# Row statistics in attention: two ScalarE passes in place of VectorE's bn_stats

## The chip, the cores and the metric

The kernel runs on one core of one Trainium2 chip. A time is the device time of one execution in microseconds (us). TensorE multiplies matrices (its rows in the profile are PE, its weight loads PEld), VectorE (DVE) and ScalarE (ACT) work element by element, GpSimd (POOL) does small operations and issues the indirect transfers, and SyncE (SP) issues the other DMAs. Each engine executes its own instructions in order and waits for others by semaphores.

## The reference

One block of a transformer over x of 8 batches x 1024 rows x 256 columns, all in float32:

```
x = x + 0.5 * ffn(layernorm(x))
x = x + attention(layernorm(x))
x = x + 0.5 * ffn(layernorm(x))
layernorm(x): (x - mean) / sqrt(var + 1e-5), over the 256 columns, no weights
ffn: a router (256 x 8, softmax, argmax) picks one of 8 experts for a row;
     an expert takes its first 320 rows, in the order of rows; the others go through a shared layer
     both are relu(x @ w1 + b1) @ w2 + b2, hidden width 1024
attention: 16 heads of width 16; xd = x @ W_down; keys, queries, values from xd per head;
     softmax(q k^T) v over the 1024 rows of a batch; out @ W_unify + b_unify
```

Each of the three layers needs the mean and the variance of every row of x as it stands then: 64 tiles of 128 rows for each layer, eight tiles in a batch.

## The kernel before, in words

**Stages.** The first feed-forward (about 0 to 660 us of the profile), the attention stage (the first exp at 659.9 us, the last at 2452.3), the second feed-forward (to 2945.7). The last blocks of the first feed-forward carry the first steps of attention beside them (`first_pair`).

**Attention** (`run`). A pair n (0 to 31) is one group of four heads of one batch: batch b = n // 4, group g = n % 4. A pair has 16 units u: for half q = u // 8 of the queries and block c = u % 8 of the keys, TensorE computes the scores of four heads (`psc`, L985, three matmuls a head, four heads on four quarters of the array's rows), ScalarE takes the exp (`ex`, L994, four a unit), and TensorE weighs the values one unit later (`av`, L1016). In the same units it computes the scores of the *next* pair in the other order (`pm`), of which VectorE takes the row maxima (`halves`, L1001, four a unit); these are subtracted in the next pair. `psc` and the projections of the next batch share four banks of PSUM, `pm` and the router's and unify's sums three others. At the end of a half VectorE turns the result (`turned`, L1031), POOL divides it (`ot`, L1039), and VectorE turns it back (`ho`, L1051).

**Work beside it.** Other work is cut into steps by Python generators, which stand in the list `beside` with a pair by which they must be done and the kind of their next step: ARRAY (TensorE), DVE or POOL. A step yields the kind of the step after it. `run` takes one step of a kind at given units: an ARRAY step where the unit is in `slots[0]` and such a step is due (this sets `other`), a DVE step where it is in `slots[1]`, a POOL step in units without an ARRAY step. The kinds with the earliest due pair go first, and `done_by(n)` takes all that is still due at a pair's end, without regard to units. The engines' order inside attention is this order of the program, written out by hand for PE, ACT and DVE; POOL and SP are ordered by the scheduler.

The generators: `prepare(b + 1)` (normed rows on POOL, transposes `ptan`, projections `pxd`, `pq`, `pv`, each evicted by ScalarE; the k and q rows go to DRAM by SP and are fetched two pairs ahead), queued when g is 0; `unify(b - 1)` (`pu`, added to x by VectorE at L1069), also when g is 0; `route(b - 1)`, the router of the second feed-forward, queued when g is 1 with four pairs' time; and `stats(b)` for batches 4 to 7, queued at the start. Batch 7 has no batch to prepare after it.

**The row statistics** (`norm_steps`, L141 on). For each of a batch's eight tiles VectorE does a bn_stats and a bn_aggr (L148, L149), one tile a DVE step; then it computes 1 / sqrt(var + eps) by a shift and four Newton steps (L156 to L173) on 128x8 numbers. `stats` calls it for attention, `route` for the router in attention, and `Layer.route` for the router outside it (the first feed-forward's, and batch 7 of the second).

**The router's steps** after the statistics: four normed tiles on POOL (`rn`), transposes (`ptrn`) and copies, the other four, logits (`pl`, L1089), then `places`: a chain of small operations between VectorE, POOL and TensorE that finds each row's slot (`places`, `behind`, `slot`, L289 to L346), and eight normed tiles with an indirect DMA each on POOL (`send`, L361), which put the rows into their slots in DRAM. For batch 6 this runs in pairs 29 to 31, and its sends follow pair 31. In the second feed-forward the tiles of the hidden layer (`h_o`, L470, L474) lie in memory that attention's pools have used.

Of the kernel before, what the change touches and what calls it, by code (L numbers as in the profile page):

```python
# [10 lines left out]
F32 = mybir.dt.float32  # L11
# [3 lines left out]
ALU = mybir.AluOpType  # L15
# [25 lines left out]
def macaron(  # L41
# [95 lines left out]

    small = ctx.enter_context(tc.tile_pool(name="small", bufs=3))

    ARRAY, DVE, POOL = 0, 1, 2  # L140

    def norm_steps(name, b, mean, rstd):


        st = small.tile([P, TB, 6], F32, tag="st", name=f"st_{name}")
        mv = small.tile([P, TB, 2], F32, tag="mv", name=f"mv_{name}")
        for t in range(TB):
            nc.vector.bn_stats(st[:, t, :], xs[b][:, t, :])  # L148
            nc.vector.bn_aggr(mv[:, t, :], st[:, t, :])  # L149
            yield DVE  # L150
        nc.vector.tensor_copy(mean, mv[:, :, 0])
        v = small.tile([P, TB], F32, tag="v", name=f"v_{name}")
        nc.vector.tensor_scalar(v, mv[:, :, 1], EPS, None, ALU.add)

        half = small.tile([P, TB], I32, tag="half", name=f"half_{name}")
        nc.vector.tensor_single_scalar(  # L156
            half, v.bitcast(I32), 1, ALU.logical_shift_right
        )
        yi = small.tile([P, TB], I32, tag="yi", name=f"yi_{name}")
        nc.vector.tensor_scalar(  # L160
            yi, half, -1.0, float(0x5F3759DF), ALU.mult, ALU.add
        )
        y = yi.bitcast(F32)
        for i in range(4):
            if i % 2 == 0:
                yield DVE
            a = small.tile([P, TB], F32, tag="a", name=f"a_{name}_{i}")
            nc.vector.tensor_tensor(a, y, y, ALU.mult)
            nc.vector.scalar_tensor_tensor(a, a, -0.5, v, ALU.mult, ALU.mult)
            to = rstd if i == 3 else small.tile(  # L170
                [P, TB], F32, tag="yn", name=f"yn_{name}_{i}"
            )
            nc.vector.scalar_tensor_tensor(to, a, 1.5, y, ALU.add, ALU.mult)  # L173
            y = to
        yield POOL

    def norm_stats(name, b, mean, rstd):
        for _ in norm_steps(name, b, mean, rstd):
            pass

    def normed(pool, tag, name, t, mean, rstd, on=None, numbered=False):
        xn = pool.tile([P, W if numbered else D], F32, tag=tag, name=name)
# [576 lines left out]
    def attention(use, weights, router):  # L759
# [318 lines left out]
        def route(b):  # L1078

            sl = slice(b * TB, (b + 1) * TB)  # L1080
            mean, rstd = router.mean[:, sl], router.rstd[:, sl]
            yield from norm_steps(f"f1_{b}", b, mean, rstd)
            logits = use.pool.tile([P, TB, E], F32, tag="logits", name=f"logits1_{b}")

            def found(q, xnt):
                pl = bank_v(f"pl_{b}_{q}")
                for i in range(4):
                    for k in range(KC):
                        nc.tensor.matmul(  # L1089
                            pl[:, i * E : (i + 1) * E],  # L1090
                            lhsT=xnt[:, k, i * P : (i + 1) * P],
                            rhs=rw_sb[:, k, :],
                            start=(k == 0),
                            stop=(k == KC - 1),
                        )
                    if i == 1:
                        yield
                nc.vector.tensor_tensor(
                    logits[:, 4 * q : 4 * q + 4, :],
                    pl[:, : 4 * E].rearrange("p (t e) -> p t e", e=E),  # L1100
                    rb_sb.unsqueeze(1).to_broadcast([P, 4, E]),
                    ALU.add,
                )
                yield ARRAY if q == 0 else DVE

            yield from rows_transposed("rn", b, mean, rstd, found)
            yield from router.places(b, logits, use.pool, bank_v, nc.gpsimd)
            for t in range(b * TB, (b + 1) * TB):
                xn = normed(
                    use.pool, "send", f"send1_{t}", t, *router.of(t), nc.gpsimd, numbered=True  # L1110
                )
                router.send(t, xn)
                yield POOL

        def stats(b):

            sl = slice(b * TB, (b + 1) * TB)
            yield from norm_steps(f"a{b}", b, amean[:, sl], arstd[:, sl])


        later = []
# [21 lines left out]

        def done_by(n):
            while any(by <= n for by, _, _ in beside):
                for kind in (POOL, DVE, ARRAY):
                    if any(by <= n and what == kind for by, what, _ in beside):
                        step(kind)

        def queue(n):  # L1150

            b, g = divmod(n, G)
            if n + 2 < PAIRS:
                fetch(n + 2)
            if g == 0:
                if b > 0:
                    beside.append([n, ARRAY, unify(b - 1)])
                if b + 1 < B:
                    beside.append([n + 1, POOL, prepare(b + 1)])
            if g == 1 and b > 0:  # L1160
                beside.append([n + 4, DVE, route(b - 1)])

        def ones(i):
            vp = use.pool.tile([P, TB * HEADS * V + S], F32, tag=f"vp{i}", name=f"vp{i}")
# [53 lines left out]
        def run(own):  # L1218
# [3 lines left out]
            ones(1)  # L1222
            for b in range(AHEAD - 1, B):
                reload(b)
                beside.append([G * (b - 1) - 1, DVE, stats(b)])
            last = None

            def weighed(parts=(0, 1)):
# [3 lines left out]
            for n in range(PAIRS):  # L1232
# [8 lines left out]
                for u in range(UNITS):  # L1241
                    todo = {}
                    old = len(later)
                    slots = SLOTS_OF[n % G < 2]
                    if ahead:
                        passes(n, n + 1, u, ORDERS[0], todo)

                        other = u % TB in slots[0] and due(ARRAY) is not None

                        whole = other or u % TB < 2  # L1250
                        weighed((0, 1) if whole else (0,))
                        passes(n, n + 1, u, ORDERS[1], todo)
                        if other:
                            step(ARRAY)
                        elif not whole:
                            weighed((1,))
                    else:

                        passes(n, None, u, ORDER_OF_LAST, todo)
                        weighed()  # L1260
                        other = False
                        if u > 1:
                            step(ARRAY)
                        if u == TB + 3:
                            beside.append([n + 1, ARRAY, islice(unify(B - 1), 2)])
                    if u % TB in slots[1]:
                        step(DVE)
                    if not other:
                        step(POOL)
                    last = (n, u, [todo["ex", h] for h in range(4)])  # L1270
                    afterwards(len(later) - old)
                    if ahead and u % TB == TB - 1:
                        lowest(n + 1, u // TB)
# [131 lines left out]
```

## Time and profile before

| | |
|---|---|
| median of 3 runs | 2952.49 us (2950.14 to 2956.28) |
| profiled execution | 2947.41 us, span 2945.7 us |
| granted TensorE clock | 0.978 (mean) |
| busy: PE, PEld | 2805.4 us (95%), 1549.6 us (53%) |
| busy: DVE, ACT, POOL | 1879.2 us (64%), 1375.5 us (47%), 863.4 us (29%) |

A line of a group reads: line of the kernel, engine, operation, tile written <- tiles read, shape, count | busy time of the group in us, mean ns of one | idle time of the engine just before them, and what ended it. A line of the waits reads: who waited <- for whom: us in total, times, longest. A line of the timeline reads: start in us, duration in us, engine, line, operation, tiles, count, and in brackets the idle time before it with what ended it.

### The profile page before, as it was taken

The numbers are of one execution on the slowest core, as the hardware profiler recorded it, in microseconds if no ns is written. First come the engines' busy times: TensorE is split into PE (matmuls) and PEld (weight loads), VectorE is DVE, ScalarE is ACT, GpSimd is POOL, SyncE is SP. The second block draws the span as 40 slices with busy tenths as digits, with TensorE's granted clock in tenths as the row PEclk, the third lists the DMA queues.
The fourth block names the chain that finished last, engine by engine and source line by source line (L and its number), as shares of the span: only waits on it lengthen the run. The fifth ranks groups of instructions, "written<-read, shape, count | busy, mean of one in ns | idle before, by whom it ended". The sixth has DMA issues, their size and how long they took to land.

```text
span 2945.7 us, 56665 instructions
## 1 busy us (share of the span) xinstructions
PE 2805.4 (95%) x22066; PEld 1549.6 (53%) x22066; DVE 1879.2 (64%) x4177; ACT 1375.5 (47%) x2512; POOL 863.4 (29%) x1144
## 2 busy tenths in 40 slices
PE   4799999899999999999999999999999998999998
PEld 4567776454444444444444444444444445666775
DVE  7344223567998888888888787788787963222221
ACT  1111111207666666766766766766765672111111
POOL 3444433314001034133123221321410215432331
PEclk7799999999999999999999999999999999999999
DMA  8522553415112101301301301301411102311440
GB/s 227 149 85 76 184 186 99 152 38 177 35 49 77 67 27 64 117 24 58 126 24 56 127 24 50 133 24 44 161 38 38 39 3 71 129 60 51 148 148 28
DMA packets 163736, 251.46 MB, mean 85 GB/s; under 512 B 36737, under 2 KB 109698, under 8 KB 163458
## 3 DMA queue, kind: packets, MB, share of 16 engines
q1 hardware_dynamic: 144178, 196.93, 20.6%
q0 software_dynamic: 18432, 50.62, 5.1%
q8 instruction: 177, 2.90, 0.4%
q14 instruction: 101, 0.83, 0.1%
q10 hardware_dynamic: 848, 0.18, 0.0%
HBM read 144.10 MB, written 103.57 MB: 84 GB/s over the span
## 4 chain that ended last, share of the span: by engine, by line
PE 63%; DVE 13%; issue 1%; POOL 1%; DMA 0%; ACT 0%; POOLq 0%; ACTq 0%
PE psc L985 19%; PE av L1016 15%; DVE halves L1001 9%; PE pm L985 7%; PE pe_o L499 5%; PE ph_o L456 5%; PE pe_e L499 2%; PE ph_e L456 2%; PE pu L1061 2%; PE pxd L860 2%; PE pv L892 1%; DVE turned L1031 1%; PE pq L878 1%; PE pl L1089 1%; PE ptrn L830 0%
## 5 line engine op out<-in xcount | busy, mean ns | idle before, releaser
L1001 DVE TENSOR_REDUCE halves<-pm 128x1 f32<-128x512 f32 x2048 | 1309.7, 681 | 258.1 <-PE pm L985 229.0
L994 ACT ACTIVATE ex<-psc 128x512 f32<-128x512 f32 x2048 | 1111.6, 596 | 579.1 <-PE psc L985 574.4
L985 PE MATMUL pm<-k,q 32*128 32x512 f32 x4096 | 872.5, 449 | 47.3 <-DVE halves L1001 38.0
L985 PE MATMUL psc<-q,k 32*128 32x512 f32 x4096 | 794.1, 456 | 2.9 <-PEq L668 2.9
L1016 PE MATMUL av<-ex,vp 128*32 128x256 f32 (+1 forms) x6472 | 614.2, 450 | 0.0
L985 PEld LDWEIGHTS psc<-q,k 32*128 32x128 f32 x4096 | 327.8, 183 | 480.5 <-issue 421.5
L985 PEld LDWEIGHTS pm<-k,q 32*128 32x128 f32 x4096 | 375.5, 184 | 129.8 <-DVE halves L1001 107.1
L985 PE MATMUL psc<-m,ones_r 32*128 32x512 f32 x2048 | 407.9, 390 | 0.0
L456 PE MATMUL ph_o<-bT_o,oa 128*128 128x512 f32 x704 | 321.9, 607 | 9.6 <-DVE h_o L474 8.5
L499 PE MATMUL pe_o<-ob,h_o 128*128 128x256 f32 x1408 | 318.6, 382 | 0.0
L1039 POOL TENSOR_TENSOR ot<-turned,rec 128x256 f32<-128x256 f32 x64 | 39.6, 619 | 886.6 <-DVE rec L1034 880.1
L499 PEld LDWEIGHTS pe_o<-ob,h_o 128*128 128x128 f32 x1408 | 265.5, 191 | 47.2 <-issue 13.5
L1016 PEld LDWEIGHTS av<-ex,vp 128*32 128x32 f32 x6472 | 129.0, 108 | 299.3 <-issue 276.3
L456 PEld LDWEIGHTS ph_o<-bT_o,oa 128*128 128x128 f32 x704 | 133.1, 194 | 164.1 <-issue 149.8
L470 ACT ACTIVATE h_o<-ph_o,ob 128x512 f32<-128x512 f32 x88 | 60.4, 687 | 338.7 <-PE ph_o L456 319.5
L474 DVE TENSOR_SCALAR h_o<-ph_o,ob 128x512 f32<-128x512 f32 x88 | 66.0, 750 | 230.4 <-ACT h_o L470 226.0
L985 PEld LDWEIGHTS psc<-m,ones_r 32*128 32x128 f32 x2048 | 197.7, 185 | 13.3
L509 DVE SCALAR_TENSOR_TENSOR y_o<-pe_o,old_o 128x256 f32<-128x256 f32 x88 | 37.2, 423 | 195.2 <-PE pe_o L499 195.1
L499 PE MATMUL pe_e<-wb,h_e 128*128 128x256 f32 (+1 forms) x640 | 143.9, 381 | 0.0
L456 PE MATMUL ph_e<-bT_e,wa 128*128 128x320 f32 x512 | 140.6, 433 | 1.8 <-ACT bT_e L204 1.8
L204 ACT COPY bT_o<-pt_bT_o 128x1024 f32<-128x1024 f32 x22 | 22.3, 1012 | 241.2 <-PE pt_bT_o L200 241.2
L499 PEld LDWEIGHTS pe_e<-wb,h_e 128*128 128x128 f32 (+1 forms) x640 | 112.9, 179 | 16.4 <-issue 3.1
(181 smaller groups left out, 2395.8 us busy)
## 6 DMA issues: line engine op xcount, KB each, us to landing
k<-krows SPq DMA_DIRECT2D x64, 512.0 KB
wa<-in_w_dram SPq DMA_DIRECT2D x16, 1024.0 KB
wb<-in_w_dram SPq DMA_DIRECT2D x16, 1024.0 KB
krows<-kh SPq DMA_DIRECT2D x32, 512.0 KB
krows<-kl SPq DMA_DIRECT2D x32, 512.0 KB
q<-qrows SPq DMA_DIRECT2D x32, 512.0 KB
rows_o<-buf SPq DMA_DIRECT2D x88, 130.0 KB
x<-in_x_dram SPq DMA_DIRECT2D x8, 1024.0 KB
```

The source lines that it names most:

```text
L456: nc.tensor.matmul(ps[:, i * 512 : i * 512 + width], lhsT=wa[:, k, (m + i) * P : (m + i + 1) * P], rhs=xnt[:, k, c0:c1], start=(k == 0), s ...
L470: nc.scalar.activation(t[:, 0, : hi - lo], ps[:, lo - c0 : hi - c0], AF.Relu, bias=bias[:, m : m + 1],)
L474: nc.vector.tensor_scalar(t[:, 1, : hi - lo], ps[:, 512 + lo - c0 : 512 + hi - c0], bias[:, m + 1 : m + 2], 0.0, ALU.add, ALU.max,)
L499: nc.tensor.matmul(ps[lo - i * P : hi - i * P, :D], lhsT=of[:, lo - a : hi - a], rhs=w[:, m, :], start=(m == 0), stop=(m == MC - 1),)
L509: nc.vector.scalar_tensor_tensor(y[:n, :], ps[:n, :D], 0.5, olds[i][:n, :], ALU.mult, ALU.add)
L860: nc.tensor.matmul(ps, lhsT=wd_sb[:, k, m * P : (m + 1) * P], rhs=xnt[:, k, :], start=(k == 0), stop=(k == KC - 1),)
L985: nc.tensor.matmul(ps, lhsT=lhs, rhs=rhs, start=(len(left) + 1 == todo[kind, h, "of"]), stop=not left,)
L994: nc.scalar.activation(ex, ps, AF.Exp, scale=S ** -0.5)
L1001: nc.vector.tensor_reduce(halves[m][:, t, half, h : h + 1], ps, AX.X, ALU.max, negate=True)
L1016: nc.tensor.matmul(avs[n, q][32 * h : 32 * h + 32, cols], lhsT=vps[b % 2][:, at : at + 2 * S], rhs=ex[:, cols], start=(c == 0), stop=(c == ...
L1039: nc.gpsimd.tensor_tensor(outs_t[q][:, :, at : at + S].rearrange("p (t a) s -> p a t s", t=4), by[:, :, :S].rearrange("p (a t) s -> p a t ...
L1061: nc.tensor.matmul(ps[:, i * D : (i + 1) * D], lhsT=outs[b, g, q][:, at : at + P], rhs=wu_sb[:, g, :], start=(g == 0), stop=(g == G // 2 - 1),
```

## The change

`norm_steps` gets an argument `junk`, a pool. Without one it is as before. With one, the sums of the rows are taken by ScalarE: eight activations with Identity over 128x256, whose accumulator gives the row sums; VectorE makes the mean and its negative of them; eight activations with Square and the negative mean as a bias per partition, whose accumulator gives the sum of squared differences. The activations' outputs go to a tile that nothing reads (tag `zero`, one buffer). They are taken two in a step of a new kind, ACT. The Newton steps on VectorE stay. `stats` of batches 4 to 7 and `route` of batches 0 to 6 pass a pool; the statistics of batches 0 to 3 for attention and those outside attention don't. `run` takes an ACT step in each unit with `other` set, behind its ARRAY and DVE steps, and in each unit of the last pair; `done_by` takes them before the ARRAY steps. `route` is now queued with an ACT step first.

```diff
-    ARRAY, DVE, POOL = 0, 1, 2
+    ARRAY, DVE, POOL, ACT = 0, 1, 2, 3
...
-    def norm_steps(name, b, mean, rstd):
-        st = small.tile([P, TB, 6], F32, tag="st", name=f"st_{name}")
-        mv = small.tile([P, TB, 2], F32, tag="mv", name=f"mv_{name}")
-        for t in range(TB):
-            nc.vector.bn_stats(st[:, t, :], xs[b][:, t, :])
-            nc.vector.bn_aggr(mv[:, t, :], st[:, t, :])
-            yield DVE
-        nc.vector.tensor_copy(mean, mv[:, :, 0])
-        v = small.tile([P, TB], F32, tag="v", name=f"v_{name}")
-        nc.vector.tensor_scalar(v, mv[:, :, 1], EPS, None, ALU.add)
+    def norm_steps(name, b, mean, rstd, junk=None):
+        if junk is None:
...
+        else:
+            total = small.tile([P, 2, TB], F32, tag="total", name=f"total_{name}")
+            lower = small.tile([P, TB], F32, tag="lower", name=f"lower_{name}")
+            for i in range(2):
+                for t in range(TB):
+                    nc.scalar.activation(
+                        junk.tile([P, W], F32, tag="zero", name=f"junk_{name}_{i}_{t}")[:, :D],
+                        xs[b][:, t, :], AF.Square if i else AF.Identity,
+                        bias=lower[:, t : t + 1] if i else 0.0, accum_out=total[:, i, t : t + 1],
+                    )
+                    if t % 2:
+                        yield ACT if t < TB - 1 else DVE
+                if i == 0:
+                    nc.vector.tensor_scalar(lower, total[:, 0, :], -1.0 / D, None, ALU.mult)
+                    nc.vector.tensor_scalar(mean, total[:, 0, :], 1.0 / D, None, ALU.mult)
+                    yield ACT
+            v = small.tile([P, TB], F32, tag="v", name=f"v_{name}")
+            nc.vector.tensor_scalar(v, total[:, 1, :], 1.0 / D, EPS, ALU.mult, ALU.add)
...
-            yield from norm_steps(f"f1_{b}", b, mean, rstd)
+            yield from norm_steps(f"f1_{b}", b, mean, rstd, use.pool)
...
-                for kind in (POOL, DVE, ARRAY):
+                for kind in (POOL, DVE, ACT, ARRAY):
...
-                beside.append([n + 4, DVE, route(b - 1)])
+                beside.append([n + 4, ACT, route(b - 1)])
...
-                beside.append([G * (b - 1) - 1, DVE, stats(b)])
+                beside.append([G * (b - 1) - 1, ACT, stats(b, own)])
...
                     if u % TB in slots[1]:
                         step(DVE)
+                    if other or not ahead:
+                        step(ACT)
                     if not other:
                         step(POOL)
```

More of the change, by code (lines that the diff above doesn't have):

```diff
@@ new lines, in norm_steps @@
+    def norm_steps(name, b, mean, rstd, junk=None):
+        if junk is None:
+            st = small.tile([P, TB, 6], F32, tag="st", name=f"st_{name}")
+            mv = small.tile([P, TB, 2], F32, tag="mv", name=f"mv_{name}")
+            for t in range(TB):
+                nc.vector.bn_stats(st[:, t, :], xs[b][:, t, :])
+                nc.vector.bn_aggr(mv[:, t, :], st[:, t, :])
+                yield DVE
+            nc.vector.tensor_copy(mean, mv[:, :, 0])
+            v = small.tile([P, TB], F32, tag="v", name=f"v_{name}")
+            nc.vector.tensor_scalar(v, mv[:, :, 1], EPS, None, ALU.add)
+        else:
+            total = small.tile([P, 2, TB], F32, tag="total", name=f"total_{name}")
+            lower = small.tile([P, TB], F32, tag="lower", name=f"lower_{name}")
+            for i in range(2):
+                for t in range(TB):
+                    nc.scalar.activation(
[9 more added lines that the diff above has]
+                    yield ACT
+            v = small.tile([P, TB], F32, tag="v", name=f"v_{name}")
+            nc.vector.tensor_scalar(v, total[:, 1, :], 1.0 / D, EPS, ALU.mult, ALU.add)
@@ L175, in norm_steps @@
         yield POOL
-    def norm_stats(name, b, mean, rstd):
-        for _ in norm_steps(name, b, mean, rstd):
-            pass
     def normed(pool, tag, name, t, mean, rstd, on=None, numbered=False):
@@ L1113, in route, with stats @@
                 yield POOL
-        def stats(b):
+        def stats(b, junk=None):
             sl = slice(b * TB, (b + 1) * TB)
-            yield from norm_steps(f"a{b}", b, amean[:, sl], arstd[:, sl])
+            yield from norm_steps(f"a{b}", b, amean[:, sl], arstd[:, sl], junk)
         later = []
```

## The prediction

> **What bounds the kernel now.** I read the page first (busy shares, then the chain that ended last), then the waits and the stretches of single head pairs in the attention stage, then rows by form, then the timeline at the places where the change acts.
>
> ```profile
> PE 2805.4 (95%) x22066; PEld 1549.6 (53%) x22066; DVE 1879.2 (64%) x4177; ACT 1375.5 (47%) x2512; POOL 863.4 (29%) x1144
> PE 63%; DVE 13%; issue 1%; POOL 1%; DMA 0%; ACT 0%; POOLq 0%; ACTq 0%
> L1001 DVE TENSOR_REDUCE halves<-pm 128x1 f32<-128x512 f32 x2048 | 1309.7, 681 | 258.1 <-PE pm L985 229.0
> L994 ACT ACTIVATE ex<-psc 128x512 f32<-128x512 f32 x2048 | 1111.6, 596 | 579.1 <-PE psc L985 574.4
> ```
>
> TensorE is busy 95% of the span and carries most of the chain; VectorE has 13% of it, nearly all through the row maxima (L1001); ScalarE has none, and its exps (L994) nearly always wait for TensorE. The whole change lies in attention (first exp at 659.9 us, last at 2452.3) and its end. Of the waits in attention, these are TensorE's for VectorE:
>
> ```profile
> PEld pm L985 <- DVE halves L1001: 91.5, 143, 1.5
> PE pm L985 <- DVE halves L1001: 37.4, 74, 1.1
> ```
>
> Stretches of three pairs (from the first exp of a pair to that of the next; columns: length, busy PE, PEld, DVE, ACT, POOL):
>
> ```profile
> 775.80:825.80 50.00, 47.77 (x548) 20.76 (x544) 47.14 (x97) 34.76 (x65) 1.24 (x2) 1.00 0.10 35
> 1164.30:1225.60 61.30, 61.14 (x576) 28.15 (x572) 47.39 (x93) 44.73 (x85) 20.34 (x23) 1.00 0.38 131
> 2403.20:2455.00 51.80, 51.80 (x386) 24.23 (x386) 8.75 (x28) 34.01 (x66) 4.16 (x13) 1.00 0.04 12
> ```
>
> Pair 2 has seven row-statistics steps on VectorE and no array work: DVE 47.1 of 50.0, near its limit. Pair 9 has six such steps but eight units with array work: TensorE is busy 61.1 of 61.3, VectorE has 14 us to spare. So the same statistics cost something in one kind of pair and nothing in the other. Pair 31 has no row maxima, and VectorE is idle.
>
> **1. What VectorE loses.** 88 steps of bn_stats and bn_aggr leave it, in eleven batches of statistics (batches 4 to 7 for attention, 0 to 6 for the router):
>
> ```profile
> L148 DVE BATCH_NORM_STATS2 st_f<-x 128x6 f32<-128x256 f32 x58 | 24.2, 417 | 0.0
> L149 DVE BATCH_NORM_AGGREGATE mv_f<-st_f 128x2 f32<-128x6 f32 x58 | 10.6, 182 | 2.0
> L204 ACT COPY bT_e<-pt_bT_e 128x256 f32<-128x256 f32 x8 | 3.0, 378 | 0.0
> L470 ACT ACTIVATE h_e<-ph_e,b 128x256 f32<-128x256 f32 x32 | 15.2, 474 | 51.7 <-PE ph_e L456 51.7
> L470 ACT ACTIVATE kept_e<-ph_e,b 128x64 f32<-128x64 f32 x32 | 10.1, 314 | 17.7 <-DVE h_e L474 17.7
> ```
>
> 88 x (0.417 + 0.182) = 52.7 us; eleven times three small operations come for two (0.17 each), so about 51 us net. What of it is on the path: a plain unit takes 2.93 us from exp to exp and holds 4 x 0.64 = 2.56 us of maxima, so VectorE has 0.37 of slack a unit. A pair without any other work would take about 48.8 us (16 x 2.93, plus 0.7 twice and 0.26 twice at the transposes of a finished half). Against that: pair 2 50.0, pair 3 51.1, pair 29 50.2: 4.9 us to gain together. Pairs 6, 10, ..., 30 (two steps and the Newton steps, 51.9 of which 1.0 is array work): about 1.0 each, 7 us. The pairs with unify, projections or router places after them: about 0.7 a batch from units at the end of a half (3.02 where a step came before, 2.93 where none did) and from work that now falls into array units: 5 us. Gain **17 us**, bounds 0 and 51.
>
> **2. What ScalarE gains.** 176 activations over 128x256, two in a slot, 88 slots; the program order puts a slot behind the unit's four exps and its array copies, and before the next unit's exps. No row has an activation with an accumulator. Main part: 0.38 (the copy of 128x256) in the first pass, 0.47 (h_e, also with a bias per partition) in the second. The read of the accumulator: the Trainium skill says of VectorE (page "VectorE: DVE Perf Modes", section "Two Vector instructions with no wait between them") that an operation that writes its accumulator out is two instructions; if ScalarE is the same, the second costs at least the fixed part of an activation: 596 - 512 x 0.833 = 0.17 (0.833 a column from 314 and 687 at 64 and 512 columns). As one instruction a slot takes 0.76 or 0.95 us, as two 1.1 or 1.3. All write one junk tile, so each waits for the one before; I take **1.1 and 1.3**, with 1.6 and 1.8 as the dear end (the read as dear as the 128x64 row and no overlap).
>
> A second rule speaks against the change. "ScalarE: Activation LUTs", section "What ACT_TABLE_LOAD costs", gives 2.66 us for each switch to another function set. Two switches a slot would make 88 x 2 x 2.66 = 468 us. The profile has one table load in all (1283 ns) under Exp, Relu and copies, and the changed program's ScalarE order holds one load too; I take 0.
>
> How much of a slot is covered is read at the unit after it. Example, behind a unit with the q projection (pair 9, unit 1):
>
> ```profile
> 1173.80 0.62 ACT L847 COPY whole<-pq 128x512 f32<-128x512 f32 x1
> 1174.28 1.13 ACT L994 ACTIVATE ex<-psc 128x512 f32<-128x512 f32 x2
> 1175.60 1.09 ACT L994 ACTIVATE ex<-psc 128x512 f32<-128x512 f32 x2 [0.19 <-PE psc L985]
> 1176.90 1.06 PE L1016 MATMUL av<-ex,vp 128*32 128x512 f32 x8
> ```
>
> The exps follow the copies with no gap, have 0.19 before the second two, and end at 1176.69, 0.21 before TensorE's weighing needs them. Cover 0.41. The medians of the same three gaps by unit, where a plain unit follows: xd projection 0.57, transposes 0.75, values 0.97, no array work 1.08, logits 1.39, unify over 2.3. Where another array unit follows, its weighing comes some 1.5 us later and all is covered. In the order of the changed kernel, slots (first, second pass) followed by a plain unit: xd 9, 11; q 7, 6; transposes 2, 3; values 7, 2; plain 1, 2. Price: 9 x 0.53 + 11 x 0.73 = 12.8; 7 x 0.69 + 6 x 0.89 = 10.2; 2.4; 1.6; 0.4. Sum **27.4 us**; as one instruction 12.2, at the dear end 54. What is late is the exp, then the weighing; TensorE executes in order, so row maxima and all later matmuls shift by the same amount.
>
> **3. The last pair.** For batch 6 no array work is due in pairs 29 and 30, so its slots are not taken there: all eight fall into pair 31, where every unit takes a slot. ScalarE's idle time in its units is 0.89: 4 x 0.21 + 4 x 0.41 = **2.5 us**. The rest of that batch's routing moves too: the transposes leave pair 30 (unit of 3.94 against 2.93) and pair 31 (3.93 against 2.96, and 0.3 for logits): **-2.3 us**.
>
> **4. The end of attention.** This moved routing now follows the last weighing, and the second feed-forward waits for it:
>
> ```profile
> 2454.04 0.72 DVE L1031 STREAM_TRANSPOSE turned<-av 128x512 f32<-128x512 f32 x1 [0.30 <-PE av L1016]
> 2456.85 0.17 DVE L343 TENSOR_TENSOR slot<-row,behind 128x8 int32<-128x8 f32 x1 [0.32 <-POOL behind L342]
> 2457.34 1.10 POOL L361 DMA_INDIRECT buf<-send,slot  x1 [0.52 <-DVE lost L345]
> 2475.76 1.27 ACT L470 ACTIVATE h_o<-ph_o,ob 128x512 f32<-128x512 f32 x2 [11.71 <-DMA buf<-send,slot]
> ```
>
> POOL's eight sends follow the slots; the hidden layer's second tile waits for them (11.7 us), TensorE behind it. So a later slot is a later everything. On the clock of before: the reciprocal root is done at 2448.9 (behind the second unify addition, 2447.6), POOL's four normed tiles at 2453.8 (4.83, as at 2386.95), transposes and copies to 2455.7, two send tiles and four more normed tiles on POOL to 2461.5, transposes, copies and logits matmuls to 2464.5, logits, top, hot 2465.5, POOL and chosen 2466.5, places 2467.1, POOL's three sums and rank to 2470.3, behind with its sums 2472.3, slot 2472.9. Against 2456.9: **+16 us**. Also queued behind: the last unify matmuls (now after behind, 2470.6), yet with 3.3 us and ph_o's 10.5 they end before the sends. Bounds: 10 (part of POOL's work ahead of the last units) and 22.
>
> **5. Moved work that costs nothing.** Router matmuls come up to eight units earlier, the projections up to two later; their number is the same. On SP's queue the first four writes of a batch's k rows go behind a fetch of k and q and an exchange of minima (and later two behind a read of minima). The fetch that reads them is due a pair (50 us) ahead and waits at most two units more; without that lead a late fetch would stop TensorE for as long. POOL's subtractions of the low halves follow the projections, and nothing waits for them but those writes.
>
> **Sum.** -17 + 27.4 + 2.5 - 2.3 + 16 = +26.6 us: 2947.41 (this execution; span 2945.7) becomes 2974.0. The median of the three runs stands 5.1 higher, 2952.49, so I predict **2979 us**, +0.9%.
>
> **The rivals.** (a) The accumulator's read comes with the instruction: slots 12.2, last pair 0.2: -17 + 12.2 + 0.2 - 2.3 + 16 = +9, 2962 us. For it: no row shows a second instruction. (b) The dear end: 54 and 6.5: +57, 3010 us. For it: two dependent operations on one junk tile. (c) The other side: VectorE is the true pace of attention, all 51 us of relief reach the path, and with (a) the sum is 51 against 26: -25, 2928 us. It decides from a relief of 26 us at cheap slots, 44 us at mine. For it: TensorE's 91.5 and 37.4 us of waits; against it: pairs such as 9, where it waits under 1 us while six steps run. (d) The end is hidden, POOL being ready earlier: +11, 2963 us.
>
> **How the numbers follow.** Mine 0.58, (a) 0.15, (b) 0.12, (c) 0.04, (d) 0.11. Mine alone holds 2966 to 2994 (0.3 us of slot either way). The range takes in (a) and (d) and reaches toward (b): 2957 to 3004. A difference of 0.2% (6 us) is about what a measurement of this kernel tells from none. Faster by more: (c), 0.04. Within: the low tails of (a) and (d), 0.06. Slower: 0.90.
>
> **What would show it.** The statistics' activations with mean near 0.4 and 0.5 us and a second short row each; pairs 13, 17, 21, 25 longer by some 3 us, pairs 2, 3, 29 near 48.8; ScalarE as a releaser of TensorE's psc and av; slot of batch 6 some 19 us after the last weighing (before: 3). I am wrong if array pairs keep their length (step 2), pair 2 stays at 50 (step 1), or h_o resumes within 22 us of the last weighing (step 4).

## The result, and the profile after

| | before | after |
|---|---|---|
| median | 2951.41 us (2948.97 to 2956.28, 5 runs) | 3051.69 us (3047.01 to 3052.96, 5 runs) |
| ratio | | 1.0335 (95% interval 1.0321 to 1.0349) |
| profiled execution, span | 2947.4, 2945.7 us | 3048.8, 3047.1 us |
| first exp; first exp of pair 31; end of the last weighing | 659.9, 2403.2, 2454.0 us | 662.1, 2489.0, 2540.0 us |
| from the last weighing to the end of the span | 491.7 us | 507.1 us |

The changed kernel is 3.3% slower. I had predicted 2979 us, with a range to 3004. Of the 101.4 us between the two spans 15.4 lie behind the last weighing (I had 16 there), 2.2 ahead of the first exp, and nearly all the rest, 82.3, between the first exp and the last, where I had expected about 11.

The page of the changed kernel: busy time by engine, the chain by engine, and the rows of the row maxima and the exps (`halves` is now L1017, `psc` and `pm` L1001, `ot` L1055, `ho` L1067).

```profile
PE 2851.0 (94%) x22114; PEld 1569.1 (51%) x22114; DVE 1846.6 (61%) x4012; ACT 1449.9 (48%) x2864; POOL 865.8 (28%) x1144
PE 61%; DVE 10%; POOL 4%; issue 2%; ACT 0%; DMA 0%; POOLq 0%; SPq 0%; ACTq 0%
L1017 DVE TENSOR_REDUCE halves<-pm 128x1 f32<-128x512 f32 x2048 | 1312.6, 683 | 328.4 <-PE pm L1001 296.2
L1010 ACT ACTIVATE ex<-psc 128x512 f32<-128x512 f32 x2048 | 1098.9, 594 | 583.3 <-PE psc L1001 571.1
```

VectorE was to be relieved, and is: 1846.6 us busy for 1879.2 (the rows of bn_stats and bn_aggr took 52.7 us in sum; part of their time lay over the ends of other rows). ScalarE has 74 us more work and still 0% of the chain. What is new in the chain is POOL, 4% for 1%, with no more busy time than before (865.8 for 863.4). An engine that does the same work and yet comes into the chain does it at another moment. The waits say who felt it (who waited <- for whom: total, times, longest):

```profile
PEld pm L1001 <- DVE halves L1017: 169.3, 207, 14.4
PE pm L1001 <- DVE halves L1017: 83.7, 71, 14.0
DVE ho L1067 <- POOL ot L1055: 58.5, 8, 13.9
```

Of the kernel before:

```profile
DVE ho L1051 <- POOL ot L1039: 1.5, 2, 0.7
```

VectorE's transpose `ho` waited for POOL's division `ot` for 1.5 us in all before; now it is 58.5 us in eight waits, 52.7 of it in six. The longest wait of TensorE for row maxima was 1.5 us; now it is 14.4. Stretches of the changed kernel: pairs 2, 9 and 12, then the third unit of pair 12 alone (u=2), then pair 31:

```profile
778.73:827.84 49.11, 46.87 (x548) 21.01 (x544) 43.94 (x79) 34.76 (x65) 1.24 (x2) 1.00 0.10 35
1175.95:1240.86 64.91, 64.90 (x580) 29.84 (x576) 45.42 (x86) 52.33 (x119) 11.49 (x11) 1.00 0.37 135
1352.19:1418.85 66.66, 57.79 (x564) 27.72 (x560) 46.67 (x79) 35.72 (x66) 20.89 (x26) 0.92 0.16 53
1361.47:1374.08 12.61, 4.81 (x40) 1.89 (x36) 3.64 (x6) 2.17 (x4) 6.65 (x9) 0.67 0.16 54
2489.03:2540.01 50.98, 49.94 (x342) 19.71 (x341) 7.76 (x29) 41.18 (x98) 7.91 (x8) 1.00 0.04 12
```

Pair 12 and its third unit in the kernel before:

```profile
1331.40:1390.68 59.28, 58.33 (x563) 28.06 (x559) 47.04 (x86) 36.69 (x69) 17.93 (x25) 1.00 0.18 64
1340.84:1344.12 3.28, 3.20 (x40) 1.33 (x36) 3.08 (x6) 2.17 (x4) 0.00 (x0) 1.00 0.24 80
```

Pair 2 went from 50.0 to 49.1 us, pair 9 from 61.3 to 64.9: much as forecast. Pair 12 went from 59.3 to 66.7, which I had not forecast, and in it one unit, which took 3.28 us before, takes 12.61 with TensorE busy for 4.81 of it. The same unit of pairs 8, 12, 16, 20, 24 and 28 takes 12.91, 12.61, 14.46, 12.84, 10.96 and 18.86 us (3.27 to 3.29 before): 63.0 us more in six units. The timeline of the changed kernel at pair 12:

```profile
1346.40 1.11 POOL L377 DMA_INDIRECT buf<-send,slot  x1 [0.53 <-DVE lost L361]
...
1365.27 1.22 POOL L200 TENSOR_SCALAR send<-x,mean,rstd 128x256 f32<-128x256 f32 x1
1366.45 0.18 POOL L202 COPY send<-number 128x4 int32<-128x4 int32 x1
1366.90 1.11 POOL L377 DMA_INDIRECT buf<-send,slot  x1 [0.28 <-POOL send L202]
...
1368.17 0.62 POOL L1055 TENSOR_TENSOR ot<-turned,rec 128x256 f32<-128x256 f32 x1
1368.83 0.71 DVE L1067 STREAM_TRANSPOSE ho<-ot 128x512 f32<-128x512 f32 x1 [7.63 <-POOL ot L1055]
...
1370.17 0.79 PE L1001 MATMUL pm<-k,q 32*128 32x512 f32 x1 [7.80 <-DVE halves L1017]
...
1371.52 1.09 ACT L1010 ACTIVATE ex<-psc 128x512 f32<-128x512 f32 x2 [8.97 <-PE psc L1001]
```

It reads from top to bottom. The router's slots are known at 1346; POOL begins its eight sends (each puts one normed tile of 128 rows into its slots by an indirect DMA), 21.6 us to 1368.0. Behind them in POOL's order stands `ot`, the division of the half that just ended. `ho` waits 7.63 us for `ot`; VectorE takes its instructions in order, so the row maxima behind `ho` wait, though their `pm` tiles were done by 1362.4; their three banks of PSUM are full, so TensorE's `pm` waits 7.80 us, and with it the scores of the running pair and the exps. In the kernel before, the `ot` of that half ran before the sends:

```profile
1333.65 0.62 POOL L1039 TENSOR_TENSOR ot<-turned,rec 128x256 f32<-128x256 f32 x1 [5.24 <-DVE rec L1034]
...
1373.48 1.09 POOL L361 DMA_INDIRECT buf<-send,slot  x1 [0.53 <-DVE lost L345]
```

Its `ho` followed at 1340.5. There, too, the sends stood in front of a division, that of the second half of pair 12, and it ran 8.4 us after the transpose that it reads, at 1401.6. Nothing waited for it: `ho` turns two groups of heads at once (there are 32 of it for 64 of `ot`), and the one that reads this `ot` came a pair later, at 1458.3. So what counts is which division the sends are in front of.

The end, beside the lines shown of before (slot at 2456.85 with the last weighing's end at 2454.0):

```profile
2558.60 0.17 DVE L359 TENSOR_TENSOR slot<-row,behind 128x8 int32<-128x8 f32 x1 [0.32 <-POOL behind L358]
2559.09 1.11 POOL L377 DMA_INDIRECT buf<-send,slot  x1 [0.53 <-DVE lost L361]
...
2577.39 1.27 ACT L486 ACTIVATE h_o<-ph_o,ob 128x512 f32<-128x512 f32 x2 [10.98 <-DMA buf<-send,slot]
```

The slot comes 18.6 us after the last weighing (2540.0) and not 2.9; `h_o` resumes 37.4 us after it and not 21.8.

### The profile page after: what moved, and what is told of

It is laid out like the page before. It is cut to its first block, busy times and chain, and to the rows that moved or that the text cites. A ratio compares the mean times of both kernels' runs of the same rounds, so it can differ in the third digit from the quotient of the medians.

```text
span 3047.1 us, 56367 instructions
## 1 busy us (share of the span) xinstructions
PE 2851.0 (94%) x22114; PEld 1569.1 (51%) x22114; DVE 1846.6 (61%) x4012; ACT 1449.9 (48%) x2864; POOL 865.8 (28%) x1144
## 4 chain that ended last, share of the span: by engine, by line
PE 61%; DVE 10%; POOL 4%; issue 2%; ACT 0%; DMA 0%; POOLq 0%; SPq 0%; ACTq 0%
PE psc L1001 19%; PE av L1032 14%; DVE halves L1017 8%; PE pm L1001 6%; PE pe_o L515 5%; PE ph_o L472 5%; PE pe_e L515 2%; PE ph_e L472 2%; PE pxd L876 2%; POOL buf L377 2%; POOL send L200 2%; PE pu L1077 1%; PE pv L908 1%; PE pl L1105 1%; PE pq L894 1%
## 5 line engine op out<-in xcount | busy, mean ns | idle before, releaser
L1017 DVE TENSOR_REDUCE halves<-pm 128x1 f32<-128x512 f32 x2048 | 1312.6, 683 | 328.4 <-PE pm L1001 296.2
L1010 ACT ACTIVATE ex<-psc 128x512 f32<-128x512 f32 x2048 | 1098.9, 594 | 583.3 <-PE psc L1001 571.1
L1001 PE MATMUL pm<-k,q 32*128 32x512 f32 x4096 | 880.9, 452 | 97.3 <-DVE halves L1017 83.7
L1001 PE MATMUL psc<-q,k 32*128 32x512 f32 x4096 | 820.9, 459 | 2.9 <-PEq L684 2.8
L1032 PE MATMUL av<-ex,vp 128*32 128x256 f32 (+1 forms) x6520 | 622.6, 452 | 0.0
L1001 PEld LDWEIGHTS psc<-q,k 32*128 32x128 f32 x4096 | 337.5, 184 | 498.7 <-issue 376.1
L1001 PEld LDWEIGHTS pm<-k,q 32*128 32x128 f32 x4096 | 376.6, 185 | 184.6 <-DVE halves L1017 169.3
L1001 PE MATMUL psc<-m,ones_r 32*128 32x512 f32 x2048 | 417.0, 392 | 0.0
L1055 POOL TENSOR_TENSOR ot<-turned,rec 128x256 f32<-128x256 f32 x64 | 39.8, 621 | 864.2 <-DVE rec L1050 839.8
L1001 PEld LDWEIGHTS psc<-m,ones_r 32*128 32x128 f32 x2048 | 205.2, 186 | 14.7
```

Of the source, the lines that this page charges most:

```text
L1001: nc.tensor.matmul(ps, lhsT=lhs, rhs=rhs, start=(len(left) + 1 == todo[kind, h, "of"]), stop=not left,)
L1010: nc.scalar.activation(ex, ps, AF.Exp, scale=S ** -0.5)
L1017: nc.vector.tensor_reduce(halves[m][:, t, half, h : h + 1], ps, AX.X, ALU.max, negate=True)
L1032: nc.tensor.matmul(avs[n, q][32 * h : 32 * h + 32, cols], lhsT=vps[b % 2][:, at : at + 2 * S], rhs=ex[:, cols], start=(c == 0), stop=(c == ...
L1055: nc.gpsimd.tensor_tensor(outs_t[q][:, :, at : at + S].rearrange("p (t a) s -> p a t s", t=4), by[:, :, :S].rearrange("p (a t) s -> p a t ...
```

## The experiments

Theory A: the stall at u=2 is the sends' place on POOL ahead of `ot`, and most of the loss. Theory B: ScalarE's slots cost more than I took.

### e1: the division of six halves on VectorE

```diff
-            nc.gpsimd.tensor_tensor(
+            on = nc.vector if g == 3 and q == 1 and 0 < b < B - 1 else nc.gpsimd
+            on.tensor_tensor(
```

> The changed kernel, with the division of the second half (ot) of pairs 7, 11, 15, 19, 23 and 27 moved from POOL to VectorE; the sends stay where they are. Theory A (POOL executes eight sends of a router's batch ahead of ot, VectorE's ho and the row maxima behind it wait): the units u=2 of pairs 8, 12, ..., 28 fall from 11 to 19 us to about 3.5, -63 us, six divisions on VectorE cost 6 x 0.4, so 3052 becomes about 2990 (2980 to 3000). Theory B (ScalarE's slots hold the exps up, at a higher price than I took): nothing changes but the six divisions, 3045 to 3056.

Measured: 2979.74 us, ratio to before 1.0117 (1.0097 to 1.0136). The six units take 3.27 to 3.34 us again, and attention, first exp to last, 68.5 us less than in the changed kernel. Theory A has it. Its waits of the same kinds:

```profile
PEld pm L1001 <- DVE halves L1017: 118.1, 211, 1.2
PE pm L1001 <- DVE halves L1017: 30.6, 67, 0.8
DVE ho L1068 <- POOL ot L1056: 5.8, 2, 5.0
```

That this is 2979.7 against a prediction of 2979 does not make the rest of the prediction right, as e5 and e6 show.

### e2 and e5: the router earlier, without any ScalarE activation

e2 edits the kernel before so that the router's statistics take two tiles in a step of VectorE:

```diff
-    def norm_steps(name, b, mean, rstd):
+    def norm_steps(name, b, mean, rstd, step=1):
...
-            yield DVE
+            if t % step == step - 1:
+                yield DVE
...
-            yield from norm_steps(f"f1_{b}", b, mean, rstd)
+            yield from norm_steps(f"f1_{b}", b, mean, rstd, 2)
```

> The kernel before, all statistics on VectorE, but the router's statistics take two tiles in a VectorE step, so that a batch's router is done four steps earlier; the order on POOL then has the eight sends ahead of ot of the second half of pairs 7, 11, ..., 27, as the changed kernel has it. No ScalarE work is added. Theory A: pairs 8, 12, ..., 28 lose 8 to 16 us each at u=2, 2951 becomes 3002 to 3020 less what the end gains by an earlier last batch (up to 12 us): 2990 to 3020. Theory B: no loss without ScalarE's slots, 2938 to 2955.

Measured: 2963.24 us, 1.0061 (1.0039 to 1.0084). A miss: the six units take 3.28, 3.60, 3.27, 3.95, 3.28 and 10.05 us. The order on POOL is that of the changed kernel, and yet only pair 28 stalls. The timeline of e2 ahead of pair 12 tells why:

```profile
1322.81 1.09 POOL L362 DMA_INDIRECT buf<-send,slot  x1 [0.53 <-DVE lost L346]
...
1344.73 1.09 POOL L362 DMA_INDIRECT buf<-send,slot  x1 [0.28 <-POOL send L187]
1345.98 0.63 POOL L1040 TENSOR_TENSOR ot<-turned,rec 128x256 f32<-128x256 f32 x1
```

The sends began 23 us ahead of `ot`, and were done when it was due (`ho` waited 0.22 us). So the order alone does no harm; it needs sends that start too late to be done and too early to be behind. e2's remaining loss lies in pairs 6 and 7 (5.0 us), in pair 28 (6.0) and in pairs that took over router work. e5 therefore moves the router by three steps and not four, which puts the slot into unit 13 and not 10, where the changed kernel has it:

```diff
-            yield DVE
+            if step == 1 or t not in (1, 3, 5):
+                yield DVE
...
-            yield from norm_steps(f"f1_{b}", b, mean, rstd)
+            yield from norm_steps(f"f1_{b}", b, mean, rstd, 3)
```

> The kernel before with all statistics on VectorE, but two tiles in three of the router's eight statistics steps, so that a batch's slot is found in unit 13 of pairs 7, 11, ..., 27, the unit in which the changed kernel finds it (e2: unit 10, and its sends were done about when ot was due). Theory A (eight sends of 22 us on POOL in front of an ot that is due some 12 us after the first): u=2 of pairs 8, 12, ..., 28 takes 8 to 16 us more, 2947 becomes 3000 to 3025, without one ScalarE activation. Theory B (it takes ScalarE's slots as well): at most what e2 lost, 2955 to 2970.

Measured: 3032.87 us, 1.0303 (1.0287 to 1.0319), a little more than expected. With every statistic on VectorE, nine tenths of the changed kernel's loss is there; u=2 takes 11.59, 10.33, 13.61, 12.62, 12.29 and 18.26 us, 59.0 us more than before. Its waits and its timeline at pair 12:

```profile
DVE ho L1052 <- POOL ot L1040: 50.4, 8, 13.3
```

```profile
1343.35 1.10 POOL L362 DMA_INDIRECT buf<-send,slot  x1 [0.53 <-DVE lost L346]
...
1363.95 0.62 POOL L1040 TENSOR_TENSOR ot<-turned,rec 128x256 f32<-128x256 f32 x1
1364.60 0.71 DVE L1052 STREAM_TRANSPOSE ho<-ot 128x512 f32<-128x512 f32 x1 [5.36 <-POOL ot L1040]
```

The cause is when the router is done, whoever takes the statistics. ScalarE's part in it is only that its slots finish them sooner.

### e3: ScalarE's passes for attention's statistics alone

```diff
-            yield from norm_steps(f"f1_{b}", b, mean, rstd, use.pool)
+            yield from norm_steps(f"f1_{b}", b, mean, rstd)
...
-                beside.append([n + 4, ACT, route(b - 1)])
+                beside.append([n + 4, DVE, route(b - 1)])
```

> The changed kernel, with ScalarE's passes for attention's statistics alone (batches 4 to 7); the router's statistics are on VectorE as before, and so the sends come behind ot again. Theory A: no stall at u=2 and no later end; 36 slots, of which some 15 stand before a plain unit at 0.5 to 0.9 us, against 1 to 5 us of relief: 2951 to 2962. Theory B: 4/11 of attention's 86 us stays, about 2982.

Measured: 2941.20 us, 0.9984 (0.9974 to 0.9994), less than either theory gave (5 us below before, where theory A had up to 11 more). Pairs 2 and 3 are 0.9 and 1.9 us shorter, `ho` waits 1.5 us in all. ScalarE's passes cost nothing on balance where they don't hurry the router. Whether the 5 us of gain are real is open: e9, below, has the same passes and does not show them.

### e4 and e8: the slots in units without array work

e4 is the changed kernel with one activation in a slot and other units for the slots:

```diff
-                    if t % 2:
-                        yield ACT if t < TB - 1 else DVE
+                    yield ACT if t < TB - 1 else DVE
...
-                    if other or not ahead:
+                    if not other:
                         step(ACT)
```

> The changed kernel, with one activation instead of two in a ScalarE slot, and the slots in the units without array work (where the plain unit after them has 1.08 us of cover against 0.62 or 0.72 for a slot). The router is then done half a pair later than in the changed kernel, and the order on POOL is that of the kernel before. Theory A: all slots are covered, the relief of VectorE (step 1) shows alone, -5 to -17, and the end is about as before: 2935 to 2950. Theory B: 176 slots each hold an exp up, 2951 + 176 x 0.3 or more, 3000.

Measured: 2964.27 us, 1.0060 (1.0043 to 1.0078): slower, where I expected faster. Not for the exps: pairs 5, 6, 10, 14, 18, 22 and 26 are 0.4 to 1.7 us shorter than before, with slots in eight to twelve of their units. It loses in four other places. ScalarE waits 3.7 us for x in pair 0, where a slot came before its load; pairs 11, 15, 23 are 2 to 3 us longer, two plain units of each half at 3.8 us; pairs 9, 13, ..., 25 are 0.8 to 1.6 us longer, with a values step at their end (4.86 us) as in e5; and pair 28 has three units of 5 us at a clock of 0.50 to 0.62. In e4 the sends come ahead of the second half's `ot` of pairs 8, 12, ..., 28, which runs 17.5 to 20.4 us late, and `ho` still waits 1.5 us in all: again a division that nothing needs soon.

The first two losses are taken away in e8, which is e4 with these changes, one of them at the end of attention:

```diff
-                    if other or not ahead:
+                    if not other and n > 0:
                         step(ACT)
...
-                    if i == 1:
-                        yield
...
+            on = nc.vector if (n, q) == (PAIRS - 1, 1) else nc.gpsimd
```

> e4 with its own losses taken away: logits in one unit (six batches x 3.5 us), no ScalarE slot in pair 0 (where x was not yet loaded, some 5 us), and ot of the very last half on VectorE, so that it does not stand behind the sends of batch 6, which run before the end of attention (-12 us of h_o's wait). 2964 becomes about 2926 (2918 to 2940), which would be faster than before; if slots in units without array work hold up exps after all, 2945 or more.

Measured: 2940.28 us, 0.9990 (0.9980 to 1.0000). That is 14 us above the forecast. The end came as forecast, 481.0 us behind the last weighing for 491.7: the slot is found at 2432.98, the last send starts at 2451.75 and `h_o` never waits for a send. In attention nothing was gained (+1.9 us): where the logits are now in one unit, the next unit is sometimes long, which e6 shows.

### e6: the logits of a half in one unit

e1 with this change:

```diff
                         )
-                    if i == 1:
-                        yield
```

> e1 with one change: the four logits matmuls of a half (pl) are issued in one unit, not two in each of two. Theory C: where the two units aren't neighbours (now unit 1 and 4, or 9 and 12), the open logits tile holds one of the three PSUM banks of the row maxima through the two units between, which take 3.8 us in place of 2.93; 24 such units x 0.85 = 20 us, so 2980 becomes about 2960 (2956 to 2967). Theory D: those units are long because of ScalarE's slots or the router's own matmuls: 2975 to 2984.

Measured: 2970.08 us, 1.0095 (1.0076 to 1.0113): 9.7 less than e1, half of what theory C gave. Stretches of the changed kernel, pair 14, the unit with the first two logits and the two behind it, which have no array work of their own:

```profile
1513.64:1517.61 3.97, 3.97 (x41) 2.24 (x44) 2.75 (x5) 2.17 (x5) 3.84 (x4) 1.00 0.05 8
1517.61:1521.42 3.81, 3.60 (x40) 1.42 (x36) 2.58 (x5) 2.17 (x5) 0.00 (x0) 1.00 0.02 4
1521.42:1525.22 3.80, 3.59 (x40) 1.41 (x36) 2.58 (x5) 2.17 (x5) 0.00 (x0) 1.00 0.00 0
```

A plain unit is 2.93. These two have its 40 matmuls at full clock and take 0.87 more, because the logits tile is open from one array unit to the next and holds one of the three banks; the third `pm` of each waits for a row maximum (0.42 us by its weight load, twice a unit). (Open means from its first matmul until VectorE has read it; the program gives the bank to no other tile till then.) The kernel before has its two logits units side by side, so that nothing lies between. In the changed kernel, in e1, e4 and e5 the router's new phase pulls them apart, for some 24 units x 0.85 = 20 us. With one unit, the long ones are gone from pairs 11, 15, 19, 23 and 27, which are 2.6 to 3.9 us shorter than in e1. The edit does more than that: the router has two array steps fewer, so its slots come in unit 10 and the projections go back to their old units (pairs 9, 13, ..., 25 are 2.3 to 2.8 us shorter, pairs 8, 12, ..., 24 1.5 to 1.8 longer). So the 9.7 us are not the open tile's alone. In pairs 10, 14, ..., 26 something else came. The same three units in e6, columns as before (the clock is the seventh):

```profile
1487.09:1491.91 4.82, 4.82 (x49) 3.15 (x52) 2.92 (x6) 2.18 (x6) 3.83 (x4) 1.00 0.05 7
1491.91:1496.89 4.98, 4.98 (x40) 2.04 (x36) 2.77 (x5) 2.17 (x5) 0.00 (x0) 0.51 0.02 3
1496.89:1500.75 3.86, 3.86 (x40) 1.71 (x40) 2.38 (x5) 2.18 (x5) 0.00 (x0) 0.75 0.00 0
```

The granted clock falls to about half in the unit behind the logits, for 1.4 to 3.8 us of loss. It does so in pairs 6, 10, ..., 26 of e6 (0.50 to 0.65), where a unit with transposes stands right before the unit with the logits. Of the other six logits units of e6, which have no such neighbour, only that of pair 7 is followed by a drop (0.71). But e8 has the two neighbours in pairs 7, 11, ..., 27 and drops in four of the six (0.50 to 0.61; not in 7 and 15), and also in four of six behind logits without that neighbour (0.56 to 0.73). What decides is open.

### e7: batch 6's router statistics on VectorE

```diff
-            yield from norm_steps(f"f1_{b}", b, mean, rstd, use.pool)
+            yield from norm_steps(f"f1_{b}", b, mean, rstd, use.pool if b < B - 2 else None)
...
-                beside.append([n + 4, ACT, route(b - 1)])
+                beside.append([n + 4, ACT if b < B - 1 else DVE, route(b - 1)])
```

> e1 with one change: the router's statistics of batch 6 are on VectorE as before, so that they are not held until pair 31. Step 4 of the prediction (its later routing is the later end): the slot comes again 3 us after the last weighing and not 19, -15.4; pairs 29 to 31 get their steps back, +5: 2980 becomes about 2970 (2966 to 2974). If the end is longer for another reason: no more than 2 us either way beside the +5, 2981 to 2987.

Measured: 2970.86 us, 1.0092 (1.0076 to 1.0108), as step 4 says. The slot is 2.9 us behind the last weighing again, and the rest takes 492.8 us for e1's 507.0.

### e11: a longer slot

e1, and in each slot behind the two activations:

```diff
+                        nc.scalar.activation(
+                            junk.tile([P, W], F32, tag="zero", name=f"more_{name}_{i}_{t}")[:, :D],
+                            xs[b][:, t, :], AF.Identity,
+                        )
                         yield ACT if t < TB - 1 else DVE
```

> e1 with one more activation of 128x256 (0.42 us, Identity, no accumulator) in each of the 88 ScalarE slots; it writes the tile that nothing reads. Step 2 of the prediction took a slot of 1.1 or 1.3 us to be longer than its cover in front of 50 plain units: these would take 50 x 0.42 = 21 us more, 2978 becomes about 2999 (2992 to 3006). If most slots are covered, as e1 against e5 suggests (pairs 9, 13, ..., 25 are 0.8 to 1.1 us apart with all else alike): 2981 to 2990.

Measured: 3011.58 us, 1.0188 (1.0162 to 1.0215), 0.71% or 21 us above e1 by the ratios (25 in attention by the two traces). So slots in units with array work do hold the exps up: an activation of 0.42 us in 88 slots is 37 us of ScalarE, and more than half of it arrives. 19.1 us of it lie in pairs 5, 9, ..., 25, eight slots each.

### e9, e10 and e12: the end of attention

e9 is e3 with `ot` of the very last half on VectorE and two tiles in a VectorE step for batch 6's router; e10 is the kernel before with these two changes; e12 is e9 with batch 6's router statistics on ScalarE. The lines that e9 adds (those of e10 and e12 differ in form):

```diff
+            yield from norm_steps(f"f1_{b}", b, mean, rstd, step=2 if b == B - 2 else 1)
...
+            on = nc.vector if (n, q) == (PAIRS - 1, 1) else nc.gpsimd
```

> e3 (ScalarE's passes for attention's statistics alone) with a change at the end: the router's statistics of batch 6 take two tiles in a VectorE step, and ot of the very last half is on VectorE. The slot of batch 6 then comes some 13 us before the last weighing and not 3 after, its sends no longer hold h_o. e8 showed 481 us from the last weighing to the end against 492. Theory: e3's gain of 4.7 and this 11: about 2931 with before at 2946 (ratio 0.9945; 0.992 to 0.997). If the gains of e3 were chance: 0.996 to 0.998.

> The kernel before with the change at the end alone (batch 6 two tiles in a VectorE step, ot of the very last half on VectorE), no ScalarE passes. Theory: -11 from the end, and some +2 in pairs 30 and 31, where e2 had the router's work one to two units earlier: 2946 becomes 2936 to 2940 (ratio 0.9975; 0.996 to 0.998).

> e9, with batch 6's router statistics by ScalarE, one activation in each unit of pairs 29 and 30 (which have no array work before the router's own), in place of VectorE two tiles at a time; the router's statistics of batches 0 to 5 stay on VectorE. Against e9 pair 29 loses its +2.3 and gains 1 (e8: -1.2), and the slot of batch 6 comes some 22 us before the last weighing. Expected: the end at 481 to 483 us, and 2 to 4 us less than e9: ratio 0.9965 (0.994 to 0.998). If a slot costs time in units without array work too: pair 29 at 50.5 or more, ratio 0.998 or more.

Measured: 2946.28 us, 0.9977 (0.9965 to 0.9990); 2946.05 us, 0.9988 (0.9975 to 1.0001); 2942.82 us, 0.9996 (0.9988 to 1.0005). Each is against its own runs of before. The end is 482.6 and 483.7 us in e9 and e10, 8 to 9 less than before, of which some 4 go in pairs 29 and 30, where the doubled steps delay row maxima. In e12 the slot came 2.6 us after the last weighing and not 22 ahead of it: with the logits in two units the router needed array steps that e8 does not, and by the order of the steps came behind unify; its end is 490.8. A difference of 0.2% is about what this kernel's runs can tell. e9 lies at its edge; none of these beats the kernel before by more. All three gained less than I had expected (0.9945, 0.9975 and 0.9965). e9's ratio is the one that I had named for the case that e3's gain was chance.

## Why the prediction was wrong

The step that failed is **step 5, "Moved work that costs nothing"**. It listed what moves on SP and three kinds of POOL and TensorE work, and left out the router's eight sends, the longest stretch that POOL has in attention. They move with the slots, from unit 10 of pair 12 to unit 13 of pair 11, and so past `ot`. Both numbers stood in the trace of before: a send takes 1.22 + 0.18 + 1.10 us and 0.28 between, 2.8 us, and with two of the eight tiles normed ahead, batch 6's sends take 19.5 us in a row; and from unit 13 to `ho` at u=1 or 2 of the next pair there are four to five units, 13 to 15 us. From these I would have estimated a stall of 4 to 7 us in each of six pairs. `ho` waited 6.0 to 9.5 us in five of them, where the sends took 20.8 to 23.4 us, each time with a wait for the transfer of an earlier send in them (2.15 us ahead of pair 12's stall), and 13.9 us in pair 28, where they took 28.1, sharing POOL with the first loads of the second feed-forward. Measured: 63.0 us at u=2, and 68.5 by what e1 takes away, the low clock behind each stall with it. No rival had it: they asked what ScalarE's slot costs, how much of VectorE's relief reaches the path, and whether the end is hidden. None of the three signs that I had named for being wrong came (array pairs that keep their length, pair 2 at 50, `h_o` within 22 us); they tested the terms that I had, and could not show one that was missing.

Part of step 5 too is that the router's matmuls come "up to eight units earlier" at no cost. They do, and their two logits units are no longer neighbours. e5 shows this without ScalarE: attention is 77.5 us longer than before, 59.0 of it at u=2, so **some 18 us** are the new order; the open tile alone would be 20 by the units' lengths, though e6, which closes it, gained only half of that. The profile of before flatters this by 6 us or so: its pair 27, at a clock of 0.89, takes 59.9 us against 54.0 in pair 23.

**Step 1** (relief -17): pairs 2, 3 and 29 came to 49.1, 49.2 and 49.1 us, near the 48.8 I named, 3.9 us of the 4.9. The 1.0 of pairs 10 to 26 is not to be seen under the open tile.

**Step 2** (slots +27.4): the mechanism is right. ScalarE's order in pair 13 of the changed kernel:

```profile
1423.78 0.43 ACT L161 ACTIVATE junk_f<-x 128x256 f32<-128x256 f32 x1
1424.10 0.20 ACT L161 ACTIVATION_READ_ACCUMULATOR junk_f<-x 128x1 f32 x1
1424.33 0.42 ACT L161 ACTIVATE junk_f<-x 128x256 f32<-128x256 f32 x1
1424.66 0.18 ACT L161 ACTIVATION_READ_ACCUMULATOR junk_f<-x 128x1 f32 x1
1424.75 2.04 ACT L1010 ACTIVATE ex<-psc 128x512 f32<-128x512 f32 x4
```

The second instruction is there, as the Trainium skill says of VectorE (page "VectorE: DVE Perf Modes", section "Two Vector instructions with no wait between them"); its row has a mean of 198 ns. (My 0.17 for its least cost took the length of an exp and the slope of other rows; the line through those rows at 64 and 512 columns, 314 and 687 ns, meets zero columns at 0.26.) The four overlap at their ends: a slot takes 0.97 us to the next exp, and 1.17 in the second pass (1454.21 to 1455.38), not 1.1 and 1.3. At these lengths my 50 exposed slots give 20.9 us. e11's 21 to 25 us for 0.42 more in each slot fit 50 to 60 of them. The one table load (1283 ns) stayed one with Identity and Square among the exps, as I had taken.

But the sum of steps 1 to 3 was too dear. e1 and e5 have nearly the same order and differ in who takes the statistics. Outside the six units u=2 e1 is 4.7 us **shorter** by the two traces, where I had -17 + 27.4 + 2.5 - 2.3 = +10.6. Pairs 9, 13, 17, 21 and 25 are only 0.8 to 1.1 us longer, where I had some 2.3 (3 less the relief at the end of a half); pairs 29 to 31, to the last exp, give 8.5 back. How much of these 15.3 us is relief and how much is cover was not separated.

**What I named as evidence for step 2 misled.** Pairs 13, 17, 21 and 25 are longer by 3.9, 3.5, 4.2 and 3.6 us, as I had said they would be. In e5, without a single slot, they are longer by 2.8, 2.4, 3.3 and 2.5. In both, one step of the xd projection has moved from the pair before into these pairs, which now have nine units with array work for eight, and the last values step stands at the end of the pair (`pv`, 5.19 us in unit 15 for 3.02), where before it was done in unit 13. By the order of the program, the sends' steps take POOL's turns when the next batch's normed rows should have begun; in e2, where the sends' steps are over earlier, the projections keep their old units. ScalarE as a releaser of TensorE, another sign that I had named, misled in part too: the weight loads of `psc` waited for exps for 85.6 us in all, 38.5 before, but 63.1 in e5. A forecast number that comes true shows a mechanism only where nothing else gives it.

**Step 3** (+2.5, -2.3): pair 30 became 2.7 us shorter, and pair 31 1.2 to its last exp (0.2 longer to the end of the last weighing): the slots at the end cost less than I took. **Step 4** (+16): 15.4 us behind the last weighing, slot at 18.6 us for 19, and e7 gives it back. This was the one step for which I had followed POOL's queue instruction by instruction.

Together: stalls 68.5 (e1), new order 18.5 (e5), statistics -4.7 (e1 against e5), in attention 82.3; from the last exp to the end of the last weighing 1.5; the end 15.4; ahead of the first exp 2.2. The stalls are shown twice, by taking them away in e1 and by making them without ScalarE in e5. The other two terms are differences of single traces, in which a low clock in one pair can be worth 6 us.

## What to carry to other kernels

When a step in a generator or a queue gets faster, list everything that it releases, to the last DMA, and lay each on its engine's queue at its new time: ask how long it takes in all and what is due behind it there. An in-order engine with much idle time (POOL at 29% here) is not a free place; 22 us in a row in front of a 0.6 us instruction that others wait for cost more than all that was saved, and the same 22 us some 9 us earlier, behind that instruction, or in front of a like one that nothing needs soon cost next to nothing. And tiles that stay open between two steps hold their bank for as long as the schedule puts between them, so a step's new phase is part of its price.

## What the runs showed that I had not expected

- An activation with an accumulator on ScalarE is followed by a read of its own, 198 ns in the mean for 128x1; with the overlap a slot of two such pairs is 0.97 us (first pass) or 1.17 (second).
- Behind a stall of 8 us the granted clock is low: 0.67 over the stalled unit of pair 12, and the next unit, with 40 matmuls at 5.66 us, at 0.83.

```profile
1374.08:1379.74 5.66, 5.66 (x40) 2.68 (x40) 3.06 (x6) 2.17 (x4) 0.00 (x0) 0.83 0.00 0
```

- The clock also fell to 0.50 without a stall, for one or two units, in the unit behind one with all logits of a half side by side (in pairs 6 to 27, 7 of 12 times in e6 and 8 of 12 in e8); what sets it off is open.
